# An audio-tower kernel: the tail tile's output projection as seven products of 64 tokens in 32-column tiles

## The chip, the cores and the metric

The kernel runs on one core of a Trainium2 chip. The metric is the device time of one execution in microseconds, as the median of three runs. All data are 32-bit floating point.

## What is computed

There are 64 sequences of 157 frames with 512 numbers each. The reference, cut to what matters:

```python
h = tok(x)                                   # frames times a 512x512 cosine basis
h = h + attn(layernorm(h))                   # values, gate, phases; ends in: total / norm @ Wo + bo
h = h + ffn(layernorm(h))                    # one of 16 experts for each sequence

def ffn(x):
    scores = softmax(mean(x, axis=1) @ Wg + bg)
    idx = argmax(scores)
    return gate * (x @ We[idx] + be[idx])
```

The attention's last step multiplies each frame's 512 numbers by the 512x512 matrix `Wo` and adds the result to `h`. The change concerns that product for one tile of the frames, and the normalisation of that tile that follows it.

## The kernel before, in words

**Tiles.** Four sequences are one group; there are 16 groups, `g` = 0 to 15, and the program goes through them in one stage each. A group's 157 frames (padded to 160) of four sequences are 640 rows, which are five tiles of 128 rows: tiles 0 to 3 and the tail tile, `TAIL`. Results of the residual stream stand in `res` (two tiles in one buffer) and `res_t` (the tail tile). Where the frames are the columns (`xT`, `gT`), the 640 columns are two halves of 320 (`HN`): two tiles and 64 columns (`HT`) of the tail tile.

**Seven products.** The 512x512 products for values (`fac_v`), gate (`fac_g`) and output (`fac_o`) use Strassen's scheme in Winograd's form: the frames' halves and the matrix's quarters are added up so that seven products do the work of eight. The sums of the frames are made by `token_sums` (L399: sums 0, 2, 1, 3 in this order, with 512 columns each, or with 640 where the tail is among them), the sums of the matrices once at the start. A product, `product` (L437), is four matmuls of 128 weights' columns by 256, twice in the profile, since each 32-bit matmul is two records: eight records at L445. `ONTO` (L426) says which products add onto a bank that another has begun: 2 onto 1, 4 onto 7, 3 onto 5. For an addition onto a bank, `room` (L428) hands out the bank that was held.

**The tail tile.** For values, `value_tail` (L490) has the scheme for the tail's two halves of 64 frames: each product is cut into matmuls of 32 columns, and four of these go to four column tiles of the array side by side (L503). For the output, `output_tail` (L795) does the plain product: four matmuls of 128x128 by 512, which are eight records at L250.

**The stage.** The order is written out by hand and kept (`manual_schedule`), so that every engine goes through its instructions as the functions at the end of the file emit them. For `g` of 2 and more: `project_and_values` (phases at L645, folded at L657; value tail, value products 1, 6, 2, 7, 5, 4, 3), `gate`, `experts_and_embedding` (experts of group `g - 1` for the tail and tiles 0 and 1, matmuls at L997; statistics of the new group), and `attention`: four `read`s (L749), the output's sums and products in the order 1, tail, 2, 6, 7, 5, 4, 3, then the experts of `g - 1` for tiles 2 and 3. Between the products stand `scale_all` (L344; multiplies the next group's columns by what `spread_deviations`, L337, has fetched from DRAM) and `value_sums`, which starts the next group's sums on GpSimd.

**After the output.** `statistics2` (L800; statistics on VectorE, the rest on GpSimd), `normal2` (L816, ScalarE, L828) and `turn_blocks` (L831, VectorE's transpose, L837) make the normalised frames; `move_blocks` (L839) moves the blocks with 16 transfers, ten of SP's queue and six of GpSimd's. In the next stage `xsum` (L864) adds the frames up, `route_own` (L875), `route_all` and `pick` choose the experts, and `fetch` (L937) loads four matrices of 1 MB through GpSimd's queue.

**Buffers.** PSUM has four tiles of two banks each; a new one takes a tile whose readers are done. The tag `u` has two buffers of 2 KB per partition, used in turn; `v_t` has one, which the tail's values and its normalised frames share before the change.

The functions that the diff touches, and what calls them:

Of the kernel before, what the change touches and what calls it, by code (L numbers as in the profile page):

```python
# [22 lines left out]
P = 128  # L23
# [30 lines left out]
def audio_tower(ctx: ExitStack, tc: tile.TileContext, a, out):  # L54
# [289 lines left out]
    def scale_all(g):  # L344

        s = S[g]
        if g == 0:
            scale = psum()
            lo = 0

            for n in (0, 1, TAIL, TAIL, 2, 3):
                rows = slice(0, P) if n != TAIL else slice(0, HT) if lo < HN - 1 else slice(HT, P)
                m, at = divmod(lo, HN)
                w = rows.stop - rows.start
                nc.tensor.transpose(
                    scale[:, m, at : at + w], s["rstd", n][rows].to_broadcast([w, P]), ident[rows, rows]
                )
                lo += w
        else:
            scale = s.pop("scale")  # L360
        for m in range(2):
            x = half(s["xT"], m)
            nc.vector.tensor_tensor(x, x, scale[:, m, :HN].unsqueeze(1).to_broadcast([P, C, HN]), ALU.mult)  # L363
# [64 lines left out]
    def room(g, i):  # L428

        held = S[g].setdefault("held", {})  # L430
        first = i not in ONTO
        ps = psum() if first else held.pop(ONTO[i])
        if i in ONTO.values():
            held[i] = ps
        return ps, first

    def product(g, i, fac):  # L437

        ps, first = room(g, i)
        ps = ps[:, :, :H]  # L440
        x, w = operand(g, i), fac[i]
        lhs = x[:, :, -2 * P :] if i in (4, 7) else x[:, :, : 2 * P]
        for b in range(2):
            for c in range(2):
                nc.tensor.matmul(  # L445
                    ps[:, b, :],
                    lhs[:, c, P * b : P * (b + 1)],
                    w[:, c, :],
                    start=(first and c == 0),
                    stop=(c == 1),  # L450
                    skip_group_check=not first,
                )
        return ps
# [36 lines left out]
    def value_tail(g):  # L490

        s = S[g]
        value_buffer(g, TAIL)
        v, ends, mids = s["v", TAIL], psum(), psum()
        top, low = slice(0, HT), slice(HT, P)
        left, right = slice(0, H), slice(H, D)

        def part(i, rows, to, cols=left, first=False):
            x, w = operand(g, i), fac_v[i]
# [15 lines left out]

        to = ends[:, 0, :H]
        together(part(1, top, to, first=True), part(5, low, to, first=True))
        for rows in (top, low):
            nc.scalar.copy(v[rows, right], to[rows])
        fourth = mids[:, 1, :P]  # L520
        together(*(part(4, rows, fourth, slice(P * n, P * (n + 1)), True) for n, rows in enumerate((top, low))))
        both = mids[:, 0, :H]
        together(part(6, top, both, first=True), part(7, low, both, first=True))
        together(part(2, top, to), part(3, low, to))
        add(v[top, right], both[top], v[top, right])
        add(v[low, left], both[low], v[top, right])
# [4 lines left out]
        add(v[top, right], to[low], v[top, right])  # L531
        nc.scalar.copy(v[top, left], to[top])
# [122 lines left out]
    def fold_phases(g):  # L655
        u = S[g]["u"]
        nc.vector.scalar_tensor_tensor(u[:, 1], u[:, 0], -1.0, u[:, 0], ALU.mult, ALU.max)  # L657
# [106 lines left out]
    def output_product(g, i):  # L764

        s = S[g]
        ps = product(g, i, fac_o)
# [11 lines left out]
        elif i == 6:  # L779
            add(first, ps, first)  # L780
            more(r12, first)
            more(r21, first)
        elif i == 7:
            add(second, ps, first)
            more(r22, second)
        elif i == 5:
            add(r22, ps, r22)
        elif i == 3:
            add(r12, ps, r12)
        elif i == 4:  # L790
            add(r21, ps, r21)
            for of in ((2,), (3,)) if last else ((2, 3),):
                statistics2(g, of)

# [21 lines left out]
    def normal2(g, n):  # L816
        s = S[g]
        if n == TAIL:
            x = p1.tile([P, D], F32, tag="v_t", name="x2_t")
# [11 lines left out]
    def turn_blocks(g, n):  # L831

        s = S[g]
        if n == TAIL:
            s["blocks2"] = p1.tile([P, C * GB, LP], F32, tag="gT", name="turned2")
# [306 lines left out]
    def project_and_values(g):  # L1142
# [3 lines left out]
        fold_phases(g)  # L1146
        value_tail(g)
        value_product(g, 1)
        keep_product(g)
        moves = move_blocks(g - 1)  # L1150
# [119 lines left out]
    def attention(g):  # L1270
# [13 lines left out]
        made = token_sums(g, tail=False)  # L1284
# [3 lines left out]
        for i in (1, 2, 6, 7, 5, 4, 3):  # L1288
            output_product(g, i)
            if i == 1:  # L1290
# [4 lines left out]
                output_tail(g)  # L1295
                statistics2(g, (TAIL,))
            elif i == 6:
# [6 lines left out]
            elif i == 5 and ahead:  # L1304
                scale_all(g + 1)
                value_sums(g + 1)
        for of in ((0, 1),) if ahead else ((0,), (1,)):
# [5 lines left out]
        elif g > 0:  # L1313
            normal2(g, 0)
            normal2(g, 1)
            next(S[g + 1]["made"])
            next(S[g + 1]["made"])
            for n in (TAIL, 2, 3):
                turn_blocks(g, n)
            expert(g - 1, 2)  # L1320
            for n in (0, 1):
                turn_blocks(g, n)
            next(S[g + 1]["made"])
# [175 lines left out]
```

## Time and profile before

| | |
|---|---|
| three runs | 1296.9, 1296.42 and 1296.0 us; median 1296.42 |
| the profiled execution | 1295.61 us |
| its span, from the first to the last instruction | 1293.8 us |
| granted TensorE clock | 0.999 |
| busy: TensorE, VectorE, GpSimd, ScalarE | 1287.2, 1042.9, 617.5, 445.8 us |
| a stage, from one output product 1 to the next | 78.30 us |
| tail tile's output, L250 with `wo`, all 16 groups | 57.5 us busy, 128 records |
| tail tile's value, L503, 14 groups | 3.03 us each on the last chain |

PE is TensorE's matmuls and PEld its loads of weights, which overlap them; DVE is VectorE, ACT ScalarE, POOL GpSimd, and SP the engine whose queue issues most transfers. A line of the groups gives the source line, the engine, the operation, what is written and read, the shapes and the count; then the busy time in us, the mean of one in ns, and the engine's idle time before it with what ended it. A line of the timeline gives the start and the duration in us, and in brackets the idle time before it. The chain in order of time has the start, the duration and what ran; it follows what ended last back to what released it.

### The profile page before, as it was taken

Reading aid. Unit: us, or ns where it says so; the run is one execution under the profiler, and the core shown is the slowest. Engines: PE = TensorE matmul, PEld = TensorE weight load, DVE = VectorE, ACT = ScalarE, POOL = GpSimd, SP = SyncE. Lnnn points to the kernel's source line nnn. Section 1 sums busy time; section 2 is a strip of 40 time slices with the busy share of each in tenths; the row PEclk is TensorE's granted clock in tenths of the full one; section 3 lists DMA queues with packets and bytes.
Section 4 is the critical chain, followed back from the end, with each engine's and each line's share of the span. In section 5 each row is a group of like instructions: output and inputs, shape, how many; then the busy total and the mean of one; then the engine's idle time right before and its main releaser. Section 6 shows DMA issues by size and latency. Waiting matters only on the chain.

```text
span 1293.8 us, 27807 instructions
## 1 busy us (share of the span) xinstructions
PE 1287.2 (99%) x10936; PEld 871.3 (67%) x10936; DVE 1042.9 (81%) x2126; ACT 445.8 (34%) x810; POOL 617.5 (48%) x795
## 2 busy tenths in 40 slices
PE   9999999999999999999999999999999999999998
PEld 5677666686666767666676666767666676666763
DVE  6889787878878788788877879788788887888573
ACT  2524334252432424334243442424324243342410
POOL 2346445354552546445454453545535554354424
PEclk9999999999999999999999999999999999999999
DMA  7015224252342425323252341524324262241507
GB/s 243 1 52 179 76 58 168 62 181 76 107 149 52 162 76 175 97 58 147 75 189 76 71 177 46 175 76 127 133 51 158 75 195 78 58 152 31 189 9 211
DMA packets 60586, 144.57 MB, mean 112 GB/s; under 512 B 14136, under 2 KB 31432, under 8 KB 52520
## 3 DMA queue, kind: packets, MB, share of 16 engines
q1 hardware_dynamic: 45620, 62.68, 17.8%
q0 software_dynamic: 14336, 79.47, 17.3%
q8 instruction: 87, 1.43, 0.5%
q10 hardware_dynamic: 500, 0.64, 0.2%
q14 instruction: 43, 0.35, 0.1%
HBM read 102.47 MB, written 20.62 MB: 95 GB/s over the span
## 4 chain that ended last, share of the span: by engine, by line
PE 97%; DMA 1%; POOL 1%; issue 1%; DVE 0%; SPq 0%; DVEq 0%; POOLq 0%
PE mm L445 29%; PE mm L997 20%; PE mm L702 17%; PE mm L749 9%; PE mm L250 6%; PE mm L503 3%; PE mm L270 3%; PE mm L272 3%; PE mm L645 3%; PE mm L681 1%; PE mm L733 1%; DMA t_v<-in_we,rows 1%; DMA wv<-in_wv 0%; PE mm L201 0%; PE mm L219 0%
## 5 line engine op out<-in xcount | busy, mean ns | idle before, releaser
L997 PE MATMUL mm<-we,x2T 128*32 128x512 f32 x2400 | 263.8, 593 | 0.0
L997 PEld LDWEIGHTS mm<-we,x2T 128*32 128x32 f32 x2400 | 74.9, 110 | 165.6 <-issue 165.5
L560 POOL TENSOR_TENSOR v<-v,bv 128x512 f32<-128x512 f32 (+1 forms) x45 | 72.7, 1631 | 136.1 <-ACT v L465 136.1
L749 PE MATMUL mm<-att,v 32*128 32x320 f32 (+3 forms) x2048 | 113.2, 357 | 0.0
L749 PEld LDWEIGHTS mm<-att,v 32*128 32x128 f32 x2048 | 94.6, 185 | 22.0 <-issue 12.6
L828 ACT ACTIVATE x<-res,shift,rstd 128x512 f32<-128x512 f32 x61 | 46.4, 807 | 179.5 <-POOL shift L244 178.7
L327 POOL TENSOR_TENSOR res<-res,bo 128x512 f32<-128x512 f32 x64 | 95.7, 1514 | 13.1 <-ACT res L323 13.0
L100 DVE TENSOR_TENSOR gT<-mm,gT 128x320 f32<-128x320 f32 (+3 forms) x128 | 71.2, 566 | 30.8 <-PE mm L702 27.7
L756 DVE TENSOR_TENSOR gT<-mm,gT 128x320 f32<-128x320 f32 x128 | 59.5, 485 | 42.4 <-PE mm L749 42.3
L232 DVE BATCH_NORM_STATS2 st<-res 128x6 f32<-128x512 f32 x128 | 87.8, 686 | 3.3
L237 POOL TENSOR_SCALAR dev<-mv 128x5 f32<-128x5 f32 (+1 forms) x20 | 4.9, 244 | 173.3 <-DVE mv L233 172.7
L445 PE MATMUL mm<-t_o,sum 128*128 128x256 f32 x384 | 85.5, 379 | 0.0
L445 PE MATMUL mm<-t_v,sum 128*128 128x256 f32 x360 | 82.4, 379 | 0.0
L720 ACT ACTIVATE gT<-gT,hbg 128x320 f32<-128x320 f32 (+1 forms) x90 | 45.6, 553 | 99.3 <-DVE gT L100 99.3
L445 PEld LDWEIGHTS mm<-t_o,sum 128*128 128x128 f32 x384 | 73.0, 190 | 9.9
L323 ACT ACTIVATE res<-res,shift,more 128x512 f32<-128x512 f32 x64 | 46.9, 803 | 87.3 <-POOL more L313 87.3
L411 POOL TENSOR_TENSOR sum<-xT 128x512 f32<-128x512 f32 (+1 forms) x30 | 25.8, 882 | 105.1 <-DVE xT L363 102.5
L951 POOL DMA_INDIRECT we<-in_we,rows x60 | 59.9, 998 | 32.7 <-DVE rows L947 16.3
L445 PEld LDWEIGHTS mm<-t_v,sum 128*128 128x128 f32 x360 | 68.4, 190 | 9.3
L237 POOL TENSOR_SCALAR rstd<-mv 128x2 f32<-128x2 f32 (+1 forms) x50 | 18.5, 370 | 114.6 <-DVE mv L233 114.5
L702 PE MATMUL mm<-sum,wg 128*128 128x320 f32 (+1 forms) x240 | 69.2, 431 | 0.0
L702 PE MATMUL mm<-xT,wg 128*128 128x317 f32 x240 | 68.9, 430 | 0.0
(236 smaller groups left out, 2983.0 us busy)
## 6 DMA issues: line engine op xcount, KB each, us to landing
xT<-in_frames SPq DMA_DIRECT2D x32, 640.0 KB
out<-res SPq DMA_DIRECT2D x236, 64.0 KB
x2T<-turned SPq DMA_DIRECT2D x150, 80.0 KB
x2T<-turned POOLq DMA_DIRECT2D x90, 80.0 KB
scale<-row SPq DMA_DIRECT2D x15, 320.0 KB
out<-res_t SPq DMA_DIRECT2D x62, 32.0 KB
out<-res_t SPq DMA_DIRECT2D x62, 26.0 KB
wg<-in_wg SPq DMA_DIRECT2D x1, 1024.0 KB
```

Source lines behind the costliest of these rows:

```text
L100: add = lambda *x: nc.vector.tensor_tensor(*x, ALU.add)
L232: nc.vector.bn_stats(st, h)
L250: nc.tensor.matmul(ps, tile_of(x[:, c], n), w[:, c, :], start=(c == 0), stop=(c == C - 1))
L323: nc.scalar.activation(s["res"][n], s["res"][n], AF.Identity, bias=shift, scale=more)
L327: nc.gpsimd.tensor_tensor(r, r, bo, ALU.add)
L445: nc.tensor.matmul(ps[:, b, :], lhs[:, c, P * b : P * (b + 1)], w[:, c, :], start=(first and c == 0), stop=(c == 1), skip_group_check=not ...
L560: nc.gpsimd.tensor_tensor(v, v, by, ALU.add)
L702: nc.tensor.matmul(ps[:, o, :width], w[:, c, o * P : (o + 1) * P], rhs[:, c, :width], start=(first and c == 0), stop=(c == 1), skip_group_ ...
L749: nc.tensor.matmul(to, s["v", n][q, c * P : (c + 1) * P], by, start=(n == 3), stop=(n == TAIL))
L756: nc.vector.tensor_tensor(th, r[:, :, 0], th, ALU.mult)
L951: nc.gpsimd.indirect_dma_start(out=ws[b][:, n * k : n * (k + 1)], out_offset=None, in_=of, in_offset=bass.IndirectOffsetOnAxis(ap=rows[:, ...
L997: nc.tensor.matmul(ps[Q * i : Q * (i + 1), :], s["x2T"][:, c, i, Q * n : Q * (n + 1)], s["ws"][i][:, c, :], start=(c == 0), stop=(c == C - 1),
```

## The change

For groups 1 to 14 (`paired`; group 0 and the last keep the old way):

- The output products come in the order 1, 4, 2, 6, 5, 7, 3. Product 4 has a bank of its own (`alone`), and VectorE's adds are spread anew: nine as before.
- The frames' sums are made with the tail among them. `output_tail_products` runs after product 3, right before the experts, with the code that the value tail has too (`tail_products`); `keep_output_tail` gathers the result ahead of and between the experts: three copies on ScalarE in all, five adds on VectorE and two on GpSimd.
- `scale_all` is split: one half after product 6, one after product 5. The next group's sums go on after the tail products.
- The tail's statistics come after the transposes of tiles 0 to 3. Its `normal2` and `turn_blocks` move into the next stage, behind value product 1 (`project_and_values`, `if g > 1`), and so before all the moves. Its normalised frames get a buffer of tag `u`.
- In all groups `fold_phases` takes the absolute value on ScalarE instead of VectorE, and stands within the value tail for groups 2 and more.

```diff
...
         row = s.pop("row").rearrange("s b t -> (s b t)")
         nc.sync.dma_start(out=scale.rearrange("p m t -> p (m t)"), in_=row.partition_broadcast(P))
-    def scale_all(g):
+    def scale_all(g, of=range(2)):
         s = S[g]
         if g == 0:
...
                 )
                 lo += w
         else:
-            scale = s.pop("scale")
-        for m in range(2):
+            scale = s["scale"]
+        for m in of:
             x = half(s["xT"], m)
             nc.vector.tensor_tensor(x, x, scale[:, m, :HN].unsqueeze(1).to_broadcast([P, C, HN]), ALU.mult)
...
     ONTO = {2: 1, 4: 7, 3: 5}
-    def room(g, i):
+    def room(g, i, alone=None):
         held = S[g].setdefault("held", {})
-        first = i not in ONTO
+        first = i not in ONTO or i == alone
         ps = psum() if first else held.pop(ONTO[i])
-        if i in ONTO.values():
+        if i in ONTO.values() and ONTO.get(alone) != i:
             held[i] = ps
         return ps, first
-    def product(g, i, fac):
-        ps, first = room(g, i)
+    def product(g, i, fac, alone=None):
+        ps, first = room(g, i, alone)
         ps = ps[:, :, :H]
         x, w = operand(g, i), fac[i]
         lhs = x[:, :, -2 * P :] if i in (4, 7) else x[:, :, : 2 * P]
...
         s = S[g]
         s["vps", n] = by_tokens(psum()[:, 0, :], s["xT"], n, wv)
-    def value_tail(g):
-        s = S[g]
-        value_buffer(g, TAIL)
-        v, ends, mids = s["v", TAIL], psum(), psum()
+    def tail_products(g, fac, keep_first, keep_fifth):
+        ends, mids = psum(), psum()
         top, low = slice(0, HT), slice(HT, P)
-        left, right = slice(0, H), slice(H, D)
-        def part(i, rows, to, cols=left, first=False):
-            x, w = operand(g, i), fac_v[i]
+        def part(i, rows, to, cols=slice(0, H), first=False):
+            x, w = operand(g, i), fac[i]
             x = x[:, :, :HT] if i in (4, 7) else x[:, :, 2 * P :]
             for c in range(2):
                 for k in (0, Q):
...
             for _ in zip(*parts):
                 pass
-        to = ends[:, 0, :H]
-        together(part(1, top, to, first=True), part(5, low, to, first=True))
-        for rows in (top, low):
-            nc.scalar.copy(v[rows, right], to[rows])
-        fourth = mids[:, 1, :P]
+        end, mid, fourth = ends[:, 0, :H], mids[:, 0, :H], mids[:, 1, :P]
+        together(part(1, top, end, first=True), part(5, low, end, first=True))
+        nc.scalar.copy(keep_first, end[top])
+        nc.scalar.copy(keep_fifth, end[low])
         together(*(part(4, rows, fourth, slice(P * n, P * (n + 1)), True) for n, rows in enumerate((top, low))))
-        both = mids[:, 0, :H]
-        together(part(6, top, both, first=True), part(7, low, both, first=True))
-        together(part(2, top, to), part(3, low, to))
-        add(v[top, right], both[top], v[top, right])
-        add(v[low, left], both[low], v[top, right])
+        together(part(6, top, mid, first=True), part(7, low, mid, first=True))
+        together(part(2, top, end), part(3, low, end))
+        return top, low, end, mid, fourth
+    def value_tail(g):
+        s = S[g]
+        value_buffer(g, TAIL)
+        v = s["v", TAIL]
+        left, right = slice(0, H), slice(H, D)
+        top, low, end, mid, fourth = tail_products(g, fac_v, v[:HT, right], v[HT:, right])
+        fold_phases(g)
+        add(v[top, right], mid[top], v[top, right])
+        add(v[low, left], mid[low], v[top, right])
         add(v[low, right], v[low, right], v[low, left])
         for n, rows in enumerate((top, low)):
             half_row = v[low, P * n : P * (n + 1)]
             add(half_row, fourth[rows], half_row)
-        add(v[top, right], to[low], v[top, right])
-        nc.scalar.copy(v[top, left], to[top])
+        add(v[top, right], end[low], v[top, right])
+        nc.scalar.copy(v[top, left], end[top])
     def keep_value(g, n):
         s = S[g]
...
     def fold_phases(g):
         u = S[g]["u"]
-        nc.vector.scalar_tensor_tensor(u[:, 1], u[:, 0], -1.0, u[:, 0], ALU.mult, ALU.max)
+        nc.scalar.activation(u[:, 1], u[:, 0], AF.Abs)
     def phasors(g, of=(0, 1)):
         u = S[g]["u"]
...
             else:
                 add(th, r[:, :, 1], th)
-    def output_product(g, i):
-        s = S[g]
-        ps = product(g, i, fac_o)
+    def output_product(g, i, paired):
+        s = S[g]
+        ps = product(g, i, fac_o, 4 if paired else None)
         (r11, r12), (r21, r22) = ([r[:, :, n : n + H] for n in (0, H)] for r in s["res2"])
         last = g + 1 == NG
         more = lambda to, x: add(to, to, x)
...
                 add_bias(g - 1, ORDER[0])
         elif i == 6:
             add(first, ps, first)
-            more(r12, first)
-            more(r21, first)
+            if not paired:
+                more(r12, first)
+                more(r21, first)
         elif i == 7:
             add(second, ps, first)
+            if paired:
+                more(r21, second)
             more(r22, second)
         elif i == 5:
             add(r22, ps, r22)
+            if paired:
+                more(r12, first)
         elif i == 3:
             add(r12, ps, r12)
         elif i == 4:
             add(r21, ps, r21)
+        if i == (7 if paired else 4):
             for of in ((2,), (3,)) if last else ((2, 3),):
                 statistics2(g, of)
+    def output_tail_products(g):
+        s = S[g]
+        kept = p2.tile([P, 2, H], F32, tag="u", name="kept")
+        s["tail"] = kept, tail_products(g, fac_o, kept[:HT, 1], kept[HT:, 1])
+    def keep_output_tail(g):
+        s = S[g]
+        r = s["res"][TAIL]
+        left, right = slice(0, H), slice(H, D)
+        kept, (top, low, end, mid, fourth) = s.pop("tail")
+        more = lambda to, x: nc.gpsimd.tensor_tensor(to, to, x, ALU.add)
+        add(r[top, right], end[low], r[top, right])
+        nc.scalar.copy(kept[top, 0], end[top])
+        add(kept[top, 1], mid[top], kept[top, 1])
+        add(kept[low, 0], mid[low], kept[top, 1])
+        for n, rows in enumerate((top, low)):
+            half_row = r[low, P * n : P * (n + 1)]
+            add(half_row, fourth[rows], half_row)
+        more(kept[low, 1], kept[low, 0])
+        more(r, kept.rearrange("p b n -> p (b n)"))
     def output_tail(g):
         s = S[g]
...
     def normal2(g, n):
         s = S[g]
         if n == TAIL:
-            x = p1.tile([P, D], F32, tag="v_t", name="x2_t")
+            paired = 0 < g < NG - 1
+            x = p2.tile([P, D], F32, tag="u", name="x2_t") if paired else p1.tile([P, D], F32, tag="v_t", name="x2_t")
         else:
             if n % 2 == 0:
                 s["x22"] = p1.tile([P, 2, D], F32, tag="v", name="x2", bufs=2)
...
     def turn_blocks(g, n):
         s = S[g]
-        if n == TAIL:
+        if "blocks2" not in s:
             s["blocks2"] = p1.tile([P, C * GB, LP], F32, tag="gT", name="turned2")
         to = s["blocks2"].rearrange("p (q c) t -> p c q t", c=C)[..., Q * n : Q * (n + 1)]
         nc.vector.transpose(to, s.pop(("x2", n)).rearrange("p (c q t) -> p c q t", c=C, q=GB))
...
         project(g)
         made = S[g].pop("made")
-        fold_phases(g)
         value_tail(g)
         value_product(g, 1)
         keep_product(g)
+        if g > 1:
+            normal2(g - 1, TAIL)
+            turn_blocks(g - 1, TAIL)
         moves = move_blocks(g - 1)
         next(moves)
         S[g - 1]["late"] = xsum(g - 1, 2 * Q, L)
...
                 for n in ((), (3, TAIL), (), ())[c]:
                     add_bo(g + 1, n)
         S[g]["blocks"] = halves(S[g]["gT"])
-        made = token_sums(g, tail=False)
+        paired = ahead and g > 0
+        made = token_sums(g, tail=paired)
         if g == 0:
             for n in (0, 1):
                 add_bo(1, n)
-        for i in (1, 2, 6, 7, 5, 4, 3):
-            output_product(g, i)
+        for i in (1, 4, 2, 6, 5, 7, 3) if paired else (1, 2, 6, 7, 5, 4, 3):
+            output_product(g, i, paired)
             if i == 1:
                 for _ in range(4 if g else 3):
                     next(made)
                 if g == 0:
                     scale_all(1)
-                output_tail(g)
-                statistics2(g, (TAIL,))
-            elif i == 6:
+                if not paired:
+                    output_tail(g)
+                    statistics2(g, (TAIL,))
+            elif i == 6 and not paired:
                 normal2(g, TAIL)
             elif i == 7 and g == 0:
                 next(made)
             elif i == 5 and g == 0:
                 value_sums(1)
                 next(S[1]["made"])
-            elif i == 5 and ahead:
-                scale_all(g + 1)
+            elif i == 6 and paired:
+                scale_all(g + 1, (0,))
+            elif i == 5 and paired:
+                scale_all(g + 1, (1,))
                 value_sums(g + 1)
+        if paired:
+            output_tail_products(g)
+            next(S[g + 1]["made"])
         for of in ((0, 1),) if ahead else ((0,), (1,)):
             statistics2(g, of)
         normal2(g, 2)
...
         if not ahead:
             normal2(g, 0)
         elif g > 0:
+            next(S[g + 1]["made"])
+            keep_output_tail(g)
             normal2(g, 0)
             normal2(g, 1)
+            turn_blocks(g, 2)
+            turn_blocks(g, 3)
+            expert(g - 1, 2)
             next(S[g + 1]["made"])
-            next(S[g + 1]["made"])
-            for n in (TAIL, 2, 3):
-                turn_blocks(g, n)
-            expert(g - 1, 2)
-            for n in (0, 1):
-                turn_blocks(g, n)
-            next(S[g + 1]["made"])
+            turn_blocks(g, 0)
+            turn_blocks(g, 1)
+            statistics2(g, (TAIL,))
             expert(g - 1, 3)
     for g in range(NG):
```

## The prediction

> **What bounds the kernel now.** I read the page's shares and slices first, then the chain that ended last, then the groups by form, then one stage in the chain's order of time and in VectorE's timeline.
>
> ```profile
> PE 1287.2 (99%) x10936; PEld 871.3 (67%) x10936; DVE 1042.9 (81%) x2126; ACT 445.8 (34%) x810; POOL 617.5 (48%) x795
> PE   9999999999999999999999999999999999999998
> PEclk9999999999999999999999999999999999999999
> PE 97%; DMA 1%; POOL 1%; issue 1%; DVE 0%; SPq 0%; DVEq 0%; POOLq 0%
> ```
>
> TensorE is busy in every slice at the full granted clock, and 97% of the last chain is its own matmuls. Its idle time, 6.6 us, lies at the start and the end. So an edit is worth what it takes from TensorE's queue, less the waits that it puts there. VectorE at 81% is no bound on average, but the order of its queue can become one.
>
> The chain in order of time, from 535 to 575 us (start, us, what), is the end of stage 6 and the start of stage 7:
>
> ```profile
> 535.65 7.12 PE mm L749 x160
> 542.78 1.92 PE mm L445 x8
> 544.70 3.43 PE mm L250 x8
> 548.14 10.36 PE mm L445 x48
> 558.50 7.00 PE mm L997 x64
> 565.50 2.15 PE mm L645 x32
> 567.65 3.03 PE mm L503 x64
> 570.68 4.51 PE mm L445 x20
> ```
>
> L250 is the tail tile's output, L503 the tail tile's value, which has the form that the output is to get. All 14 stages that change show the same 3.43. A stage lasts 78.30 us (product 1 starts at 464.41, 542.71 and 621.01), with no TensorE wait.
>
> **What TensorE gains.** Removed per stage: 8 records of 512 columns, 3.43 us. Added: 32 matmuls, 64 records, as in L503 x64: 3.03 us (four tiles at once: 0.864 for products 1 and 5, 0.436 for product 4, 0.864 each for 6 and 7 and for 2 and 3; together 3.028). Changes of tile shape cost 0.09 to 0.10 each (product 3 to the experts took 1.82 where a product takes 1.73), and their number stays. Difference 0.40 us; 14 stages (1 to 14) make 5.6.
>
> A rule speaks against this. The Trainium skill, "TensorE: Matmul & The Clock Gate", Part 3 (packing small matmuls), measured 3.07x from four tiles at once, not 4x; the estimate from it is 3.03 x 4/3.07 = 3.94 us, 0.5 more than what is removed, so 7 us slower. This trace decides: a quartet of L503 starts every 0.216 us, and a full product of the same 256 columns (L445) takes 0.216 per record, so here four tiles run at 4x.
>
> **What VectorE gets.** Its timeline before, in the same stage:
>
> ```profile
> 544.37 0.49 DVE L100 TENSOR_TENSOR gT<-mm,gT 128x320 f32<-128x320 f32 x1
> 544.96 0.69 DVE L411 TENSOR_TENSOR sum<-gT 128x512 f32<-128x512 f32 x1
> 548.17 0.69 DVE L100 TENSOR_TENSOR res_t<-mm,res_t 128x512 f32<-128x512 f32 x1 [0.59 <-PE mm L250]
> 551.63 0.69 DVE L100 TENSOR_TENSOR u<-mm,u 128x512 f32<-128x512 f32 x1 [0.96 <-PE mm L445]
> 555.69 2.88 DVE L363 TENSOR_TENSOR xT<-xT,scale 128x1280 f32<-128x1280 f32 x2
> ```
>
> Removed: the tail's add (0.69; one follows another every 0.61) and fold_phases (0.48). Added: two 128-element sums (0.28, at a pitch of 0.2), two sums of 640 instead of 512 (+0.1 each), five small adds as in the value tail (rows 424 and 290 ns, about 1.65 together). Net +1.2 us; the products need nine adds either way. VectorE idles 4.3 us between 548 and 583, so the sum fits; the order must be walked. Product 1 starts at 542.71, its successors come every 1.73 (the first after 1.83).
>
> - **Product 4, now second.** Its second matmul reads the half of gT that the add of 544.37 writes, ended 544.86. TensorE loads weights one record ahead, so it wants the data at 544.76. The delay is 0.10 plus a wake-up of some 0.05 (VectorE starts 0.04 to 0.10 after what it waited for), less the 0.11 by which a load just after a wait is followed sooner by its matmul (after 542.71 the next record comes in 0.32, not 0.43). I take 0.05 us a stage; the bounds are 0 and 0.2.
> - **Product 6** starts at 548.0 and loads the third sum's result from 547.8; the sums start at 544.96, 545.57, 545.77, 546.38, 546.58 and that one ends at 547.4. Margin 0.4. Before, the tail's 3.43 us lay there.
> - **Product 3** goes on product 5's bank, after VectorE has read it. The walk: product 4's add 548.1, product 2's 548.7, product 6's (wants TensorE) 549.9, the first half of scale_all 550.5 to 552.0, product 5's until 552.7. Product 3 starts at 553.2 and loads from 553.0. Margin 0.3.
> - **Tail products** run 555.0 to 558.0, the experts to 565.0, the value tail 567.1 to 570.2. Expert 2's bank was read at 555.3. The five adds come at 561.2 to 562.9, the transposes behind them to 564.1, expert 2's result at 564.7, the other transposes to 566.7, the tail's statistics to 567.6, expert 3's result to 568.3, which value product 1 wants at 570.2. Here VectorE waits for GpSimd's last add (565.3 at the latest), and expert 3's result is queued behind that wait.
> - **Next stage.** ScalarE normalises the tail after value product 1, at 573.0 to 573.8. VectorE, with the transpose, both xsum (1.61 and 1.13) and product 6's add, comes to product 7's add at 577.8, ended 578.5; product 4, which goes on that bank, loads at 578.7. Margin 0.2, and the same for product 5's add before product 3. Routing is ready at 579.6, wanted at 580.4.
>
> **What lies beside other work, at nothing.** On ScalarE, 34% busy: two copies and one (0.37 each, L519 and L532), the tail's 0.81 moved, and Abs. No row shows Abs; the nearest are Tanh on the same 128x320, 0.53, and the Sin rows, 0.47. A table load (1.28 by the rows) would bound it from above; the program has none more, and even that would end at 570.7, ahead of the 572 at which the next copy can start. On GpSimd, 48%: one 128x512 add (1.27 to 1.51) and one on half the rows (no row; 0.3 to 0.7). What hides them is its idle time from 567 to 576; without that cover they would hold back the moves. Such adds slow VectorE: L991 takes 970 ns beside L327 and 746 in the tail's form, so I allow 0.2 in a place with 1.9 to spare. The moves of x2T wait for the tail's transpose, 574.4 instead of 567.7. SP's ten then run to about 580.7 (577.4 before); behind them SP holds only stores that come at 610. GpSimd's six, the fold and the four weight fetches behind them stay at 578 and 584, as GpSimd comes to them no sooner before. The matrix is wanted at 602, the fetched weights are in at 598.
>
> **Sum.** 0.40 - 0.05 = 0.35 us a stage, x14 = 4.9. The profiled execution took 1295.61 (span 1293.8 and 1.8 around it), so it would take 1290.7; the runs' median, 1296.42, lies 0.8 higher: 1291.5. With 0 and 0.2 at product 4: 1290.8 and 1293.6.
>
> **Rivals.**
> - **VectorE's order eats the gain.** In the next stage 0.2 are to spare. The tail's transpose has been put between the value tail's adds and the sums of the router; if ScalarE or the sums come 0.5 later than in my walk, product 4 and product 3 of the values wait 0.3 a stage: 4.2 us back, 1295.7. For it: the margin is thin in three places and each is a sum of ten durations. Against it: the same rows in the same order fixed the walk, and TensorE's delay there gives VectorE its time back.
> - **The scale comes too late: slower.** VectorE comes to scale_all at 550.5 instead of 555.7, ahead of product 5's add. The transfer is issued 1.5 to 4.7 us after product 1's start in stages 1 to 13 and took about 3.2 to its last packet (issued 545.84, traffic ended at 549.0), so it lands at 4.7 to 7.9 after the start; VectorE comes at 7.8, and with product 3's 0.3 a delay counts from 8.1. The worst stage lies just inside. The point from which it decides: told 2.5 us later than packets end, the median stage (6.0) loses 0.4 and the gain is gone; at 3.5 later it loses 1.4: 1296.4 - 4.9 + 13 x 1.4 = 1310. Against it: that delay would be as long as the transfer.
> - **The tiles do not run at 4x** beside these operands, as the skill's figure has it: 1296.4 + 7 + 0.7 = 1304. Against it: L503 has the same shapes, tiles and kind of operands.
>
> **How the numbers follow.** The forecast, 1291.5, has 0.70; the same with nothing lost at product 4, near 1290.8, 0.10; VectorE's order 0.14; the late scale 0.04; the tiles 0.02. A measurement of this kernel can tell 0.2%, 2.6 us, from no change. The first case stays faster than 1293.8 in all its bounds; of VectorE's order a little does, most is within 0.2%, and a part, with longer delays, is slower. Faster 0.79, same 0.13, slower 0.08. The range reaches from 1290.2 (no wait, and the runs' own spread) into VectorE's order: 1295.0.
>
> **What would show it.** Right: L250 keeps only stage 0's and 15's output, L503 shows 128 records a stage with 3.03 us for each half, a stage lasts 77.95, and the only TensorE wait is some 0.05 ahead of product 4. Wrong: a stop of TensorE's loads for VectorE at product 3 or 6, or in the next stage at products 4 and 3; VectorE waiting for a transfer at L363; tail records starting further apart than 0.216 a quartet.

## The result, and the profile after

| | before | after |
|---|---|---|
| median of 22 runs each | 1296.47 us (1295.65 to 1298.47) | 1293.76 us (1292.53 to 1296.05) |
| the profiled execution, its span | 1295.61, 1293.8 us | 1293.44, 1291.6 us |
| an undisturbed stage | 78.30 us | 77.94 us |
| stages longer than that, of 13 whole ones | 0 | 8, by 0.14 to 0.34 us |

The ratio is 0.9977 (95%: 0.9971 to 0.9984): faster by 2.7 us, where 4.9 were forecast. TensorE is still the bound at the full clock. VectorE has 29 us more to do (2.1 a stage where the prediction's sum has 1.2), GpSimd 32, ScalarE 22; the page's shares and its last chain say:

```profile
PE 1283.5 (99%) x11720; PEld 874.6 (68%) x11720; DVE 1071.7 (83%) x2194; ACT 467.8 (36%) x868; POOL 649.9 (50%) x823
PEclk9999999999999999999999999999999999999999
PE 97%; DMA 1%; POOL 1%; issue 0%; SPq 0%; DVE 0%; POOLq 0%
```

The last chain in order of time, from the end of one stage into the next, answers to the one shown of before (start, us, what). Line numbers have moved: L749 is L754 now, L997 L1032, L645 L650, L503 L500.

```profile
612.76 7.12 PE mm L754 x160
619.88 12.33 PE mm L445 x56
632.21 3.17 PE mm L500 x64
635.37 6.87 PE mm L1032 x64
642.24 2.15 PE mm L650 x32
644.39 3.03 PE mm L500 x64
647.42 4.73 PE mm L445 x21
```

L250 is gone from the stage. The seven output products take 12.33 where they took 1.92 + 10.36 = 12.28; the tail and the experts behind it take 3.17 + 6.87 = 10.04 where 3.43 + 7.00 = 10.43 stood. Together 0.34, and by the stages 0.36.

Where are the other two microseconds? Between the first output product of stage 1 and that of stage 15, the profile of after is 3.41 us shorter than that of before, which is 14 x 0.36 = 5.04 less 1.64 for the longer stages. Its start was 0.45 longer than in the profile of before (79.81 to the first output product) and its end 0.82 longer (a transfer of weights, `t_v<-in_we,rows`, came later). Start and end moved as much from kernel to kernel in all the profiles below (78.7 to 80.1, 60.9 to 61.7), whatever was changed in the stages; so I do not count them as the change's. The 1.64 lie in the stages.

Putting every matmul of a longer stage beside its like in an undisturbed one shows one stop in each: in seven stages 0.14 to 0.21 us ahead of gate product 4 (1.30 together), in the twelfth 0.32 ahead of the tail's expert (0.34 with what follows). The waits of the weight loads name the seven (us in total, times, longest):

```profile
PEld mm L707 <- DVE gT L100: 2.9, 7, 0.4
```

Gate product 4 goes onto product 7's bank, so VectorE must have gathered product 7, that is, added it to `gT`. Its timeline in such a stage (start, us, and in brackets the idle time and what ended it), then ScalarE's in the same stage, in one without a stop, and in the kernel before:

```profile
355.78 0.18 DVE L233 BATCH_NORM_AGGREGATE mv<-st 128x2 f32<-128x6 f32 x1
357.65 0.40 DVE L100 TENSOR_TENSOR res<-mm,sines 128x128 f32<-128x128 f32 x1 [1.70 <-ACT res L293]
...
359.05 0.18 DVE L233 BATCH_NORM_AGGREGATE mv<-st 128x2 f32<-128x6 f32 x1
359.15 0.85 DVE L100 TENSOR_TENSOR gT<-gT,mm 128x512 f32<-128x512 f32 x2
```

```profile
353.01 0.64 ACT L293 COPY res<-mm 128x256 f32<-128x256 f32 x1
356.00 0.94 ACT L725 ACTIVATE gT<-mm,hbg 128x317 f32<-128x317 f32 x2 [2.35 <-PE mm L272]
356.83 0.27 ACT L292 COPY sines<-mm 128x129 f32<-128x129 f32 x1
356.98 0.65 ACT L293 COPY res<-mm 128x256 f32<-128x256 f32 x1
```

```profile
275.07 0.64 ACT L293 COPY res<-mm 128x256 f32<-128x256 f32 x1
277.04 0.94 ACT L725 ACTIVATE gT<-mm,hbg 128x317 f32<-128x317 f32 x2 [1.33 <-PE mm L707]
278.12 0.27 ACT L292 COPY sines<-mm 128x129 f32<-128x129 f32 x1
278.29 0.64 ACT L293 COPY res<-mm 128x256 f32<-128x256 f32 x1
```

```profile
590.52 0.94 ACT L720 ACTIVATE gT<-mm,hbg 128x317 f32<-128x317 f32 x2 [1.33 <-PE mm L702]
591.41 0.27 ACT L292 COPY sines<-mm 128x129 f32<-128x129 f32 x1
```

Start with ScalarE. Its tanh (L725; L720 in the kernel before) of gate product 2 normally starts 2.34 us after that product's first matmul (0.2 after the next product has begun), after an idle 1.33. In seven stages it starts 1.0 us later. Its program waits there for TensorE's semaphore alone, the signal that the product is done. In the trace that semaphore rises late, 0.02 before the tanh, although the matmuls themselves are not shifted by 0.01. Behind the tanh, in order, stands ScalarE's copy of embedding tile 1 (L293); VectorE has the statistics of that tile next in its queue and stands idle 1.70 us; behind these stands the gathering of product 7, done 0.06 before gate product 4 can start instead of 0.72.

The stage without a stop is not quite undisturbed either. Its copy L292 of tile 1 starts 3.42 us after gate product 2's first matmul (274.70), that of the kernel before 3.23 (588.18): TensorE's next signal, for tile 1, rises at 3.35 instead of 2.98. It is late, by 0.35 or more, in every whole stage of the changed kernel but the twelfth, and that is why VectorE has 0.72 to spare there and had 0.92 before. Where the tanh is 1.0 late, this signal follows within 0.08 us of the tanh's own. Two things were open: whether this queue is what stops TensorE, and what of the change makes TensorE's signals late.

### The profile page after: what moved, and what is told of

It reads as the page before. It is cut to its first block, busy times and chain, and to the rows that moved or that the text cites. A ratio compares the mean times of both kernels' runs of the same rounds, so it can differ in the third digit from the quotient of the medians.

```text
span 1291.6 us, 29529 instructions
## 1 busy us (share of the span) xinstructions
PE 1283.5 (99%) x11720; PEld 874.6 (68%) x11720; DVE 1071.7 (83%) x2194; ACT 467.8 (36%) x868; POOL 649.9 (50%) x823
## 4 chain that ended last, share of the span: by engine, by line
PE 97%; DMA 1%; POOL 1%; issue 0%; SPq 0%; DVE 0%; POOLq 0%
PE mm L445 30%; PE mm L1032 20%; PE mm L707 18%; PE mm L754 9%; PE mm L500 7%; PE mm L270 3%; PE mm L272 3%; PE mm L650 3%; PE mm L250 2%; PE mm L686 1%; PE mm L738 1%; DMA tables<-in_table_sums 1%; DMA t_v<-in_we,rows 1%; PE mm L201 0%; PE mm L219 0%
## 5 line engine op out<-in xcount | busy, mean ns | idle before, releaser
L1032 PE MATMUL mm<-we,x2T 128*32 128x512 f32 x2400 | 263.5, 592 | 0.1
L1032 PEld LDWEIGHTS mm<-we,x2T 128*32 128x32 f32 x2400 | 77.0, 110 | 163.0 <-issue 160.3
L754 PE MATMUL mm<-att,v 32*128 32x320 f32 (+3 forms) x2048 | 113.2, 357 | 0.0
L411 POOL TENSOR_TENSOR sum<-xT 128x512 f32<-128x512 f32 (+1 forms) x30 | 29.0, 989 | 165.9 <-PE mm L500 163.4
L754 PEld LDWEIGHTS mm<-att,v 32*128 32x128 f32 x2048 | 94.6, 185 | 22.0 <-issue 12.6
L725 ACT ACTIVATE gT<-gT,hbg 128x320 f32<-128x320 f32 (+1 forms) x90 | 45.6, 556 | 93.7 <-DVE gT L100 93.7
L707 PE MATMUL mm<-sum,t_g 128*128 128x317 f32 x240 | 68.9, 430 | 0.0
```

Source lines behind the costliest of these rows:

```text
L707: nc.tensor.matmul(ps[:, o, :width], w[:, c, o * P : (o + 1) * P], rhs[:, c, :width], start=(first and c == 0), stop=(c == 1), skip_group_ ...
L754: nc.tensor.matmul(to, s["v", n][q, c * P : (c + 1) * P], by, start=(n == 3), stop=(n == TAIL))
L1032: nc.tensor.matmul(ps[Q * i : Q * (i + 1), :], s["x2T"][:, c, i, Q * n : Q * (n + 1)], s["ws"][i][:, c, :], start=(c == 0), stop=(c == C - 1),
```

## The experiments

Theory A: TensorE's gain is 0.36 a stage as walked, and of the missing 1.64 us the 1.30 in the gate are VectorE's queue behind ScalarE's late tanh. The rivals: the value stage, where the forecast had its thin margins (B), ScalarE's new work, the order of the output products, the scaling. In the comparisons "after" is 1293.76; each kernel's ratio is to runs of the kernel before on the same chip. Experiments 1 to 4 ran on one chip, 5 to 8 on a second, 9 to 12 on a third; for the changed kernel no chip is on record.

**1. Statistics of embedding tile 1 behind gate product 7's gathering** (on VectorE; TensorE's order unchanged).

```diff
             for n in {6: (0,), 2: (1,), 3: (2, 3, TAIL)}.get(i, ()) if ahead else ():
                 embed(g + 1, n)
-                embed_statistics(g + 1, n)
+                if n != 1:
+                    embed_statistics(g + 1, n)
+            if i == 7 and ahead:
+                embed_statistics(g + 1, 1)
```

> Changed kernel with one edit in the gate stage: the sums and statistics of embedding tile 1 are queued on VectorE behind the gathering of gate product 7 instead of ahead of it; TensorE's order is the same. Theory A (the new stops of 0.14 to 0.21 us ahead of gate product 4 arise because VectorE stands in its queue behind ScalarE's late copy of embedding tile 1): the stops go, all stages last 77.94 us, and the time falls by 1.3 to 1.6 us, from 1293.8 to about 1292.3. Theory B (the stops come from VectorE having too much work in the value stage, or from TensorE itself): the stops stay, 1293.8 within 0.4.

Measured: 1292.53 us, ratio 0.9969 (0.9958 to 0.9980). Every stage lasts 77.94 but the twelfth (78.26). The tanh was late in even more stages, 11 of 13; VectorE's timeline in one of these:

```profile
355.13 0.18 DVE L233 BATCH_NORM_AGGREGATE mv<-st 128x2 f32<-128x6 f32 x1
357.10 0.89 DVE L100 TENSOR_TENSOR gT<-gT,mm 128x512 f32<-128x512 f32 x2 [1.78 <-PE mm L707]
357.90 0.38 DVE L100 TENSOR_TENSOR res<-mm,sines 128x128 f32<-128x128 f32 x1
```

The gathering now waits for TensorE's product 7 only, and is done 1.05 us ahead of product 4 in all 13 stages. The ratio's interval overlaps the changed kernel's; it is the stages that show the queue to be what stopped TensorE in the gate. What makes the tanh late, and the twelfth stage's stop, are not touched by it.

**2. The absolute value back on VectorE** (`scalar_tensor_tensor` at its old place instead of `nc.scalar.activation(..., AF.Abs)`).

> Changed kernel with one part undone: the absolute value of the projections is taken by VectorE again, at its old place ahead of the tail's value products. Theory A: the gate stage is later than this by 30 us and ScalarE waits there for TensorE's signal, so the stops stay as they are; VectorE loses about 0.6 us at the start of the value stage, where value product 1's gathering has a margin under 1 us; 1293.8 to 1295. Theory B (ScalarE's extra work is what makes its tanh late): the stops go, 1292.3.

Measured: 1293.2, ratio 0.9977 (0.9969 to 0.9986). Neither: an ordinary stage grew to 77.98, since value product 4 came 0.04 late in each and 0.25 in one; the tanh was over 0.4 late in three stages only, with one stop in the gate. Tile 1's signal was late in all 12 stages (the twelfth left out). So Abs on ScalarE is worth 0.04 a stage, and its removal shifted the routing by 0.27 us (VectorE writes `rows` 41.24 us after output product 1 instead of 40.97). That the tanh answered to so small a shift pointed to a meeting of two events.

**3. Before, with the moved normalisation alone** (the diff's `normal2(g - 1, TAIL)` and `turn_blocks(g - 1, TAIL)` behind value product 1, and their buffer).

> Kernel before with one part of the change alone: the tail's normalisation and its turn go to the next value stage, behind value product 1, into the other buffer; the tail's output stays as 16 direct products next to output product 1. Theory A: TensorE's work is unchanged and value product 4 has the margin found in the changed kernel (0.38 us), so 1296.5 within 0.5, and the gate stage keeps its margin of 0.9 us ahead of product 4. Theory B (the moved normalisation is what makes VectorE late): stops of 0.1 to 0.2 us in the gate stage already here, 1297 to 1298.5.

Measured: 1298.36, ratio 1.0015 (1.0008 to 1.0022): theory A's number fell, B's came. Nine of 13 tanhs are about 1.0 late, and the loads wait:

```profile
PEld mm L702 <- DVE gT L100: 3.8, 9, 0.5
```

But not in the value stage: the stops, 0.13 to 0.23, are all ahead of gate product 4, but for one of 0.3 at the tail's expert. This part of the change, then, makes the loss, without the tail's products. What it moves against TensorE is the routing and all that GpSimd issues after it: the gathers of the experts' weights begin 41.62 after output product 1 instead of 41.16, and the gather of the bias row (`be`) is issued 1.36 us after gate product 2's first matmul instead of 0.90.

**4. The old order of the output products**, 1, 2, 6, 7, 5, 4, 3, and the scaling whole behind product 5.

> Changed kernel with one part undone: output products in the old order 1, 2, 6, 7, 5, 4, 3, product 4 again added onto product 7 in PSUM, the scaling of the next input whole and behind product 5; the tail's Strassen products stay last. Theory A: TensorE has the same work and the new order buys little; 1293.3 to 1294.8. Rival (the old order leaves VectorE too late for the next stage's inputs, which is what the new order is for): each of 14 stages gains a stop ahead of the projections of 0.3 to 1 us, 1298 to 1308.

Measured: 1311.83, ratio 1.0121. Both were wrong on the place. Product 2 goes onto product 1's bank and had 3.43 us of the tail's output ahead of it in the kernel before; now it follows at once:

```profile
PE mm L445 <- ACT u L778: 10.2, 14, 0.7
```

TensorE waits 0.73 us a stage for ScalarE's copy of product 1, and a little for product 6's sums; 1.31 us a stage are lost, all among the output products. Product 4, second and on its own bank, is the cover that the tail's output was.

**5. The bias gather issued 6 us later.** In the changed kernel it is issued on GpSimd over the end of gate product 2 (whose first matmul starts at 352.64), in the kernel before it is over by then (first matmul at 588.18):

```profile
353.99 0.96 POOL L1016 DMA_INDIRECT be<-in_be,expi  x1 [0.18 <-DVE even L100]
```

```profile
589.08 1.00 POOL L981 DMA_INDIRECT be<-in_be,expi  x1 [0.18 <-issue]
```

```diff
                 pick_gate(g - 1)
-                bias(g - 1)
...
             if i == 5:
+                bias(g - 1)
```

> Changed kernel with one edit: in the gate stage GpSimd issues the gather of the experts' bias row behind its three additions to the values instead of ahead of folding the next input, some 6 us later. TensorE's and VectorE's order is the same. Theory A1 (ScalarE's tanh of gate product 2 is late by 1.0 us because that issue, 0.96 us long, now begins 1.36 us after product 2's first matmul and so lies over product 2's end at 2.13; in the kernel before it began at 0.90 and was over by 1.86): no tanh is late, all stages but the twelfth last 77.94, 1292.3. Theory A2 (the gather of the experts' weights, which flows at that time at 300 to 400 GB/s, delays the signal): the tanh is late in 7 to 11 of 13 stages as before this edit, the stops stay, 1293.8.

Measured: 1291.66, ratio 0.9960 (0.9947 to 0.9974). All stages last 77.94, the twelfth too, and no tanh is late in 13; VectorE is done 0.91 ahead of product 4. GpSimd and ScalarE:

```profile
352.59 0.93 POOL L986 DMA_INDIRECT we<-in_we,rows  x1 [0.30 <-issue]
...
353.68 1.54 POOL L122 TENSOR_TENSOR xT<-xT 128x640 f32<-128x640 f32 x1
...
360.13 0.97 POOL L1016 DMA_INDIRECT be<-in_be,expi  x1
```

```profile
354.83 0.94 ACT L725 ACTIVATE gT<-mm,hbg 128x317 f32<-128x317 f32 x2 [1.33 <-PE mm L707]
```

The weights' gathers are where they were, so their traffic alone is not the cause (A2 falls). One reservation: in none of the four kernels on this chip is any signal of gate product 2 or tile 1 late, and the changed kernel as it is has no run on record there. Experiment 11 has the same answer on a chip where signals were late.

**6. Both edits of the gate stage.**

> Changed kernel with both edits of the gate stage: the statistics of embedding tile 1 behind the gathering of gate product 7 on VectorE, the issue of the bias gather behind the additions to the values on GpSimd. All theories: stages of 77.94 as with the first edit alone, 1292.5 within 0.5; under theory A1 no tanh is late and VectorE keeps at least 0.9 us ahead of gate product 4.

Measured: 1291.11 us (1290.6 to 1291.67), ratio 0.9955 (0.9941 to 0.9968). All stages 77.94, no late tanh, 1.05 us ahead of product 4. It is faster than both kernels, and its interval, alone among the faster kernels', is clear of the changed kernel's; what it has over the edit of the bias alone lies within the spread of their starts.

**7. Before, with the statistics behind product 7.**

> Kernel before with the edit in the gate stage alone: statistics of embedding tile 1 behind the gathering of gate product 7 on VectorE. Theory A: the stages of before last 78.30 without a stop and have nothing to give back, 1296.6 within 0.5. Rival (the edit gains by itself, whatever the tail does): 1295 or less.

Measured: 1296.36, ratio 0.9999 (0.9991 to 1.0008), all stages 78.30. The edit gains only what the change had lost.

**8. The scaling whole behind product 5**, all else as in the changed kernel.

> Changed kernel with one part undone: VectorE scales both halves of the next input behind output product 5, instead of the first half behind product 6. Theory A: VectorE is caught up by the tail's products, the stages last 77.94 but for the stops in the gate, 1293.8 within 0.5. Rival (the split is what keeps VectorE in time for the next stage's tail products and value product 1): a stop of 0.2 to 0.7 us in each of 13 stages, 1296.5 to 1303.

Measured: 1319.16, ratio 1.0174: slower than the changed kernel by 25.4 us, 1.95 in each of 13 stages, more than the rival's bound. VectorE's timeline after output product 1, first with the scaling whole, then in the changed kernel:

```profile
398.27 0.69 DVE L100 TENSOR_TENSOR u<-mm,u 128x512 f32<-128x512 f32 x1 [0.51 <-PE mm L445]
400.00 0.69 DVE L100 TENSOR_TENSOR res<-mm,res 128x512 f32<-128x512 f32 x1 [1.03 <-PE mm L445]
...
404.73 2.49 DVE L100 TENSOR_TENSOR res<-res,u 128x512 f32<-128x512 f32 x2
```

```profile
314.79 0.69 DVE L100 TENSOR_TENSOR u<-mm,u 128x512 f32<-128x512 f32 x1 [0.51 <-PE mm L445]
315.39 1.48 DVE L363 TENSOR_TENSOR xT<-xT,scale 128x1280 f32<-128x1280 f32 x1
...
320.12 1.29 DVE L100 TENSOR_TENSOR res<-res,u 128x512 f32<-128x512 f32 x2
```

The half that stood in front of product 5's add filled 1.03 us in which VectorE now idles; and two adds behind the scaling take 2.49 instead of 1.29, beside GpSimd's sums. That is 2.2 us, and VectorE's queue is full from there to the value products: TensorE loses 0.2 each at the projections and at the value tail, 0.96 at value product 2 (a wait of 0.68) and 0.46 at value product 4 (a wait of 0.20).

**9. Before, with GpSimd held up for 0.65 us ahead of the bias gather.**

```diff
+                nc.gpsimd.tensor_tensor(idle, idle, idle, ALU.add)
                 bias(g - 1)
```

> Kernel before with nothing of the change: one addition of 128x128 zeros on GpSimd, about 0.46 us, is put ahead of the issue of the bias gather in the gate stage, so that this issue begins 1.36 us after gate product 2's first matmul, where it begins in the changed kernel. Theory A1 (the place of that issue alone makes the tanh late): the tanh comes about 1.0 us late in at least 7 of 13 stages, TensorE stops 0.1 to 0.25 us ahead of gate product 4 in them, 1297.3 to 1298.8. Theory A3 (it takes something else of the change, the moved normalisation for example): no tanh is late, all stages 78.30, 1296.4.

Measured: 1296.28, ratio 0.9999; no tanh late, all stages 78.30. The addition took more than the 0.46 assumed, so the issue began at 1.55 and not at 1.36: the run says that 1.55 is harmless there, and does not test 1.36.

**10. Before, with the moved normalisation and the bias gather 6 us later.**

> Kernel before with the moved normalisation of the tail, as run already, and the issue of the bias gather behind GpSimd's additions to the values. Theory A1 (what the moved normalisation cost there is only the meeting of that issue with gate product 2's end): the stages are back at 78.30, 1296.4 within 0.5. Theory B (the move costs of itself): 1298 again.

Measured: 1296.80, ratio 1.0002 (0.9994 to 1.0010), all stages 78.30, no tanh late. So what the moved normalisation cost in experiment 3 was that meeting in the gate; the two ran on different chips.

**11. The bias gather one place later, behind the folding.**

> Changed kernel with the issue of the bias gather only one place later on GpSimd, behind the folding of the next input: it would begin about 2.9 us after gate product 2's first matmul and end at 3.9. Theory A1: the issue begins after product 2's end at 2.13, so no tanh is late and all stages last 77.94. Theory A4 (the gather's issue delays whatever product ends near it): the lateness moves to embedding tile 1's copies or to product 7's gathering, 78.0 to 78.2 in most stages.

Measured: 1291.32 in one run, issue at 2.90, no tanh late; the stages last 77.94 but for the twelfth, 78.26. A step of 1.5 us is enough.

**12. The tail's products twice.**

> Changed kernel with the tail's 64 output records issued twice (the first set is overwritten by the second, the output is unchanged): the price of the set where nothing else is moved. Theory A (four records of 32 columns run side by side at the pitch of one full record, 3.03 us for 64): each of 13 paired stages grows by 3.0 to 3.1 us, to 80.97. Rival (the Trainium skill's 3.07 times for four tiles in TensorE: Matmul & The Clock Gate, Part 3): 3.03 x 4 / 3.07 = 3.95 us, stages of 81.9.

Measured: 1333.92 in one run. The paired stages last 80.97 (the twelfth 81.31), 3.03 more each, and the chain has:

```profile
649.48 6.19 PE mm L500 x128
```

6.19 less 3.17 are 3.02 us for 64 records beside nothing else. Although the issue began at 1.36 here too, only one tanh was late, by 0.24; but tile 1's signal was late in all 12 stages, by 0.27 to 0.37.

**What the twelve say of the late signals together** (start of the bias gather's issue after gate product 2's first matmul; tile 1's signal is due at 2.98; the twelfth stage, in which the issue starts 0.1 to 0.9 later, left out):

| issue starts | kernels | tanh late by 0.9 or more | tile 1's signal late |
|---|---|---|---|
| 0.90 | before, 7 | 0 of 24 (one by 0.5) | 0 of 24 |
| 1.36 | after, 1, 3, 4, 12 | 36 of 60 (four by 0.3) | 60 of 60 |
| 1.57 | 2 | 1 of 12 (two by 0.5) | 12 of 12 |
| 1.55 to 1.57 | 8, 9 | 0 of 24 | 0 of 24 |
| 2.9 and later | 5, 6, 10, 11 | 0 of 48 | 0 of 48 |

In the 72 stages of rows two and three tile 1's signal rises 0.93 to 1.17 us after the gather's issue has ended. With 1.36 the issue ends at 2.29 to 2.33, just where the tanh's signal is due (2.31); that signal then came in time in 20 stages, up to 0.3 late in four, and together with tile 1's in 36.

## Why the prediction was right in sign and short in size

- **TensorE's gain: right.** Stages of 77.94 against 77.95 forecast. The quartets do run at 4x: 3.02 us were measured for the set alone, 3.03 were taken. The Trainium skill's 3.07x ("TensorE: Matmul & The Clock Gate", Part 3), measured there for four row tiles of 512 columns and not for column tiles as here, would have made it an estimated 3.94; the row decided rightly, and the rival built on the rule falls.
- **Product 4's wait: right.** The seven products take 12.33 instead of 12.28: 0.05.
- **Products 6 and 3, the tail, value products 4 and 3: right in outcome.** No stop; in the stage that I measured through, TensorE's next use came 0.64, 0.56, 0.38 and 0.42 after what it waits for (0.4, 0.3, 0.2, 0.2 walked). Value product 1 was closer than walked: 0.69 instead of 1.9.
- **"VectorE's order eats the gain": the kind was right, the place wrong.** It was put at value products 4 and 3, with 4.2 us. VectorE's order cost 1.30 us, in the gate; the other 0.34 are the twelfth stage's. That 1293.8 lies in the range is in part luck: its upper end was set for stops that did not come.
- **The step that failed: "Routing is ready at 579.6, wanted at 580.4", where the walk ended.** Only TensorE was asked who wants it. Fetches and bias stayed where they were (41.25 after output product 1; 41.16 before), as forecast; but TensorE had come 0.36 nearer, and against it the issue of the bias gather moved from 0.90 to 1.36. The gate stage was taken to be caught up and was not walked; VectorE had 0.92 us to spare ahead of gate product 4, and the late tanh takes 1.0. Without the meeting (experiments 5, 6 and 11) the kernel takes 1291.1 to 1291.7, which the sum had as 1291.5; two of these ran on the second chip.
- **The scale's arrival:** no wait for the transfer at L363 appeared, so that rival fell; but its price was of the right size. It counted a delay of VectorE past 0.3 in full; experiment 8's 2.2 us cost 1.95.
- **What lies at nothing on ScalarE and GpSimd:** Abs, the copies and GpSimd's adds stopped nothing (Abs in its new place even gains 0.04).

What stays open: why TensorE's signals are held back. That the place of the issue matters is shown best on one chip, the third: with 1.36 (experiment 12) tile 1's signal was late in 12 of 12 stages, with 2.9 (11) and 7.7 (10) in none of 24, though 12 has the doubled tail besides. The start alone does not decide: at 1.57 the signal was late in all stages of 2 and in none of 8, which ran on another chip; and in the twelfth stage of before and of 7 the issue starts at 1.35 and the tanh is on time. Whether the chip or something else in these kernels makes that difference wasn't tried.

The stop of the twelfth stage, at the tail's expert, came in eight of the nine kernels whose bias gather started 1.36 to 2.9 us after that product in the other stages (0.3; in 2 and 8 0.5; not in 9), and in none with 0.90 or over 7. The load waits there for ScalarE's copy of the embedding (L293); why that is late wasn't followed.

## What to carry to other kernels

When TensorE becomes faster by a little, everything that did not move has moved against it: look at each wait in the following stages that had less margin than the new phase can cost, not only at those near the edit. In an in-order queue put what TensorE wants next ahead of what waits for a third engine; moving one group of statistics behind one gathering took away the stops in the gate, with the signal still 1 us late in 11 of 13 stages. And before an instruction is taken out from between two dependent ones, ask what it covered: here a direct product of 3.43 us had hidden a copy, and the split of one VectorE operation filled a gap worth 25 us.

## What the runs showed of the hardware that was not expected

- TensorE's completion signals came late although the matmuls ran on time: in all 72 stages of six kernels in which GpSimd's gather was issued 1.36 or 1.57 us after a product's first matmul, the signal due at 2.98 rose 0.27 to 0.66 us late, and in 37 of them the one ahead of it, due at 2.31, by 0.9 or more. In two other kernels with 1.55 to 1.57 none was late. The cause is open.
- A stop of TensorE ahead of a 128x128 product cost more than its length: the record after the stopped one comes 0.37 instead of 0.27 us behind it in the gate. In one stage of experiment 3 a stop of 0.021 us cost 0.125.
- VectorE's adds of 128x512 took up to 1.63 us instead of 0.68 beside GpSimd's sums (experiment 8).
